# Two transformer blocks on one core: softmax totals from a column of ones, and outputs kept by tokens

## The chip, the core and the metric

The kernel runs on one core of one Trainium2 chip. The metric is the device time of one execution in microseconds (us). A core has five engines that this text speaks of: PE (TensorE, matmuls, with its weight loads shown apart as PEld), DVE (VectorE), ACT (ScalarE), POOL (GpSimd) and SP (SyncE, which issues most of the DMAs). PE writes its results to PSUM[...]; DVE and ACT read them there[...].

## The reference

The input `x` is 4 sequences (batch B = 4) of S = 1024 tokens with D = 128 features. Two blocks follow each other, each adding `s * g` to the residual stream `x`: `s` is an attention of 16 heads of 8 features, `g` is the silu of a feed-forward network, and both read the same layernorm of `x`. Cut to what matters:

```python
def block0_attention(x):             # causal window of 64 tokens
    k, q, v = split(x @ w_kqv)
    score = q @ k.T / sqrt(D) + alibi_bias        # -inf outside the window
    return softmax(score) @ v                     # by head

def block0_ffn(x):                   # an expert mixture per sequence
    g  = (relu(x @ gate_w1.T + gate_b1) @ gate_w2.T + gate_b2).mean(axis=1)
    W1 = W1 + sum_e g[e] * TW1[e];  b1 = b1 + g @ Tb1      # per sequence
    W2 = W2 + sum_e g[e] * TW2[e];  b2 = b2 + g @ Tb2
    return gelu(x @ W1.T + b1) @ W2.T + b2

def block1_attention(x):             # over the batch: 4 positions, 1024 columns
    q, k, v = x @ Wq.T + bq, x @ Wk.T + bk, x @ Wv.T + bv
    probs = softmax(q @ k.T + gate(q) * position_bias)
    return (probs @ v) @ Wo.T + bo

def block1_ffn(x):
    h = silu(x @ w1.T * w1_s) * (x @ w2.T * w2_s)
    h = gelu(h @ h1.T * h1_s)
    h = gelu(h @ h2.T * h2_s)
    return h @ w3.T * w3_s

xn = layernorm(x); x = x + block0_attention(xn) * silu(block0_ffn(xn))
xn = layernorm(x); x = x + block1_attention(xn) * silu(block1_ffn(xn))
```

All matmuls are in fp32.

## The kernel before

**Tiling.** The tokens are cut into eight units u of U = 512 tokens, two to a sequence. Activations lie by features: 128 features on the partitions, tokens along the free axis. Each unit goes through the first block (attention in four blocks t of 128 queries, and the feed-forward `hid0` and `out0`), then a residual step and a second layernorm, then the second feed-forward (`gated`, `hidden` twice, `out1`). The second attention mixes the four sequences, so it waits for the last of them and runs in eight slices of 128 columns (`attend`, steps with a star) beside unit 7.

**Order.** PE, ACT and DVE execute exactly the order of a long string, `ORDER`: each word is a step, a letter and its arguments, written out by hand. `q` projects queries, keys and values; `m` and `v` evacuate them; `s`, `b`, `x`, `o` are scores, bias, exponential, weighting of a block; `d` divides a pair of blocks by their totals; `A` to `E` are gates and the mixing of expert weights (`E` is one of 16 DVE steps for a sequence); `f`, `g` the first feed-forward; `r` the residual; `l` and `t` the statistics of first and second layernorm, `n` its scaling, `k` its way back to features; `w`, `h`, `i`, `j` the second feed-forward; `y` the last output. A step with several words per unit does a quarter of the work in each. POOL and SP are placed by the framework.

**Block-0 attention.** The scores of 16 heads stand in one PSUM tile of four banks, `ps_S` (L393). DVE adds bias and mask (L410), ACT takes the exponential without a maximum (L741; a second version of the program, with the maximum, exists behind a flag and isn't run here). `weighted` makes two sets of matmuls into `ps_O`: the value products (L438: 32 per block, each 64 queries, the 32-column stationary window of `vb` holding one head's 8 value columns per head group between zeros), and the softmax totals (L451: 16 or 32 per block, with a constant 0/1 matrix `totals` as stationary operand). Both come out by features: row = head and feature, column = query. `divided` takes the reciprocal of all 128x256 totals (L462) and multiplies (L463).

**Layernorm.** Its statistics need tokens on partitions. The first reads a second copy of the input that is loaded by tokens (`in_xt`, kept in `g1`), while `x` holds the copy by features. The second (`ln_mid`) turns `x` on PE by four transposes (L224, tile `ps_T`) first. `ln_back` (L231) turns the scaled tokens back to features for the matmuls.

**Outputs.** `out0` (L481), `out1` (L536; L531 in two halves for unit 7) and the second attention's `project_out` (L666) have the weights as stationary operand and 512 tokens moving past. Their results are by features, so biases and scales are per-partition operands of the ACT or DVE instruction that evacuates them.

**PSUM.** Besides `ps_S` there are three single-bank buffers `ps_M`, taken in turn by nearly all other matmuls, and one bank with the tag O for `ps_O`, `ps_T` and `ps_V`.

Of the kernel before, what the change touches and what calls it, by code (L numbers as in the profile page):

```python
# [29 lines left out]
C_ID, C_MP, C_SEL, C_EXP, C_TOT, C_TOF = np.cumsum([0, 128, 4, 64, 256, 128]).tolist()  # L30
C_N = C_TOF + 128
# [3 lines left out]
for _name, _n in (  # L35
    ("gb1", 1), ("gb2", 8), ("b1", 4), ("b2", 1), ("bq", 1), ("bk", 1), ("bv", 1), ("bo", 1),
    ("gW", 8), ("gb", 8), ("ga", 1), ("pb", 4), ("w1s", 4), ("w2s", 4), ("h1s", 4), ("h2s", 4), ("w3s", 1),
):
    VEC[_name] = (sum(n for _, n in VEC.values()), _n)
V_N = sum(n for _, n in VEC.values())  # L40


def constants():
# [13 lines left out]


    tot = np.tile((r[None, :] // 8 == g[:, None]).reshape(1, P), (P, 1))
    c[:, C_TOT:C_TOT + P] = tot  # L60
    c[:, C_TOF:C_TOF + P] = tot * (p[:, None] < W)
# [24 lines left out]

ORDER = """
    l1 n10
    q0 m03 m00 m01 z m02 s00 b00 k10 A00 A01 s01 B0 b01 v00 C0 D0 E0 v01 s02 v03 x01 E0 E0 v02 E0 E0 x00 b02
    o00 s03 E0 x02 E0 l3 E0 E0 b03 o01 E0 f0 d01 E0 f1 E0 x03 E0 f0 f0 E0 E0 f1 E0 l2 o02 o03 n30 f0 d03 n20  # L90
    g0 g0
    q1 v11 k20 k30 r0 t0 f1 m11 A10 n01 m12 g1 k01 v10 f1 v13 w0 m13 g1 m10 v12 w0 w0 s10 A11 b10 w0 s11 x10
    b11 x11 h0 h0 s12 o10 b12 o11 s13 b13 h0
    q2 d11 x12 h0 o12 B1 x13 C1 D1 E1 E1 E1 E1 i0 E1 o13 E1 d13 i0 E1 E1 i0 E1 E1 r1 i0 E1 E1 t1 E1 f2 E1 j0
    v20 v23 j0 f2 f2 E1 m21 m20 E1 n11 g2 v21 f2 k11 m22 g2 v22 w1 m23 w1 s20 w1 b20 w1 h1 l4 x20 h1 s21 n40
    o20 b21 x21 h1 o21 s22 d21 b22 h1 x22 l5 i1 i1 s23 b23 o22 x23 n50 i1 i1 o23 j1 j1 k50 f3 d23
    q3 r2 t2 m31 n21 f3 k40 f3 v31 f3 g3 m30 A20 k21 v32 v33 g3 w2 v30 w2 m32 m33 w2 A21 s30 b30 w2 x30 B2
    h2 s31 o30 b31 C2 x31 h2 s32 o31 D2 h2 E2 b32 h2 x32 E2 i2 d31 i2 E2 o32 E2 E2 E2 s33 E2 E2 b33 E2 x33
    E2 i2 E2 i2 E2 o33 E2 d33
    q4 f4 r3 E2 E2 m43 E2 f4 j2 v40 t3 n31 f4 m41 f4 j2 g4 k31 v42 m40 v43 g4 w3 w3 m42 l6 v41 w3 w3 s40 b40  # L100
    n60 h3 x40 h3 s41 b41 o40 k60 l7 n70 h3 x41 h3 k70 s42 o41 b42 i3 f5 i3 s43 b43 d41 x43 x42 i3 i3 o42
    o43 j3 d43 j3 r4
    q5 t4 f5 m53 f5 n41 A30 m51 m50 f5 v51 g5 k41 g5 v53 w4 m52 v52 v50 w4 w4 s50 b50 w4 x50 A31 h4 h4 B3
    o50 s51 b51 C3 x51 h4 D3 E3 E3 E3 s52 b52 E3 E3 E3 E3 o51 x52 h4 i4 d51 s53 b53 E3 E3 E3 E3 o52 x53 i4
    i4 E3 i4 o53 d53 E3 r5 j4 f6 E3 E3
    q6 f6 t5 m61 E3 f6 m63 f6 n51 v60 j4 v61 g6 k51 g6 v62 w5 m62 v63 w5 m60 w5 w5 s60 b60 h5 x60 h5 s61 o60
    b61 x61 h5 h5 o61 s62 i5 i5 b62 d61 x62 i5 s63 b63 x63 i5 o62 o63 d63 f7 r6 f7 j5 f7 t6 j5 n61 f7
    q7 k61 m71 m70 g7 v70 v73 v71 w6 m72 g7 m73 w6 v72 *A0 w6 s70 *B0 b70 *V0 w6 s71 b71 x70 h6 *A1 *b0 s72
    b72 x71 *C0 *E0 *B1 *N0 x72 o70 h6 *b1 *D0 o71 *A2 d71 *V1 *C1 *B2 o72 s73 *E1 *N1 h6 *G0 b73 *F0 *b2 h6
    *D1 x73 *C2 i6 *E2 o73 i6 *G1 d73 r7 *Y0 *A3 *N2 t7 *V2 *B3 *D2 *b3 n71 *V3 i6 i6 *C3 *E3 *F1 k71 j6 *N3  # L110
    *Y1 w7 *G2 *D3 j6 w7 w7 *A4 *F2 *G3 *F3 *Y2 *Y3 y60 *V5 *B4 *b4 *A5 *A6 w7 *V6 *V4 *C4 *B5 *E4 *b5 *V7
    h7 *B6 *A7 h7 *b6 *N4 *C5 *B7 *b7 *D4 h7 *C7 *E5 h7 *G4 *E7 *F4 *N5 *Y4 *D5 *G5 i7 *C6 *E6 *N6 i7 *F5
    *N7 *D6 *Y5 i7 *D7 *G6 i7 *F6 *G7 j7 *Y6 j7 *F7 y70 *Y7 y71
# [4 lines left out]
def block_kernel(ctx: ExitStack, tc: tile.TileContext, a: dict, out: bass.AP):  # L118
# [20 lines left out]

    x = main.tile([P, B, S], F32, tag="x", name="x")  # L140

    g1 = main.tile([P, B, S], F32, tag="g1", name="g1")
    xt = [g1[:, b, :].rearrange("p (i d) -> p i d", d=P) for b in range(B)]
# [7 lines left out]
    tb = const.tile([P, FC + 1, E], F32, tag="tb", name="tb")  # L151
# [6 lines left out]
    nc.scalar.dma_start(out=g1[:, 0, 0:U], in_=a["xt"][:, 0:U])  # L158
    nc.sync.dma_start(out=wqkv, in_=a["wqkv"])
    nc.sync.dma_start(out=cst, in_=a["const"])  # L160
    nc.scalar.dma_start(out=g1[:, 0, U:S], in_=a["xt"][:, U:S])
# [15 lines left out]
    totals = [cst[:, at:at + P].rearrange("p (g c) -> p g c", g=4) for at in (C_TOT, C_TOF)]  # L177
# [7 lines left out]
    DVE.memset(vb[:, 0:2328], 0.0)  # L185
    POOL.memset(vb[:, 2328:24 + 9 * 512], 0.0)
    slots = vb[:, 24:24 + 9 * 512].rearrange("p (m h q) -> p m h q", m=9, h=H)[:, :, :, 0:HD]

    def tokens(u):

        b, c = u // 2, (u % 2) * U
        return b, slice(c, c + U)

# [21 lines left out]
    def ln_in(u):  # L215

        return ln_stats(xt[u // 2][:, 4 * (u % 2):4 * (u % 2) + 4, :])

    def ln_mid(u):

        b, cx = tokens(u)
        turned = ps.tile([P, 4, P], F32, tag="O", name="ps_T")
        for i in range(4):
            PE.transpose(turned[:, i, :], x[:, b, cx.start + i * P:cx.start + (i + 1) * P], ident)  # L224
        return ln_stats(turned)
# [32 lines left out]

    one = const.tile([P, 1], F32, tag="one", name="one")
    POOL.memset(one, 1.0)  # L260
    in_order = {mybir.EngineType.PE, mybir.EngineType.Activation, mybir.EngineType.DVE}
    with tc.manual_schedule(engines=in_order | {mybir.EngineType.Pool}):
        steps = bound()

        for i in range(3):
            PE.matmul(bank(), lhsT=vb[:, 0:P], rhs=vb[:, 0:U], start=True, stop=True)
            if i == 1:
                next(steps)
        scale = ln_in(0)
        next(steps)  # L270
        fast = nc.values_load(flag[0:1, 0:1], min_val=0, max_val=1)
        ln_back(0, scale())

    def program(exact):
# [41 lines left out]
        def gates_c(b, gr):  # L316
            shares = small([P, FC + 1, E], "shares")
            DVE.tensor_tensor(shares, tb, gr.unsqueeze(1).to_broadcast([P, FC + 1, E]), ALU.mult)
            mb = at.tile([P, FC + 1], F32, tag="mb", name="mb", bufs=2)
            DVE.tensor_reduce(mb, shares, AX.X, ALU.add)  # L320
            DVE.tensor_tensor(mb, mb, v("b1", 0, FC + 1), ALU.add)
            own = [at.tile([P, F], F32, tag=f"mw{j}", name=f"mw{j}", bufs=2) for j in range(2)]
            mixed[b] = (own[0], own[1], mb)

# [27 lines left out]
        def qkv(u):  # L352
# [26 lines left out]
            def value(i):  # L379
                copy = DVE.tensor_copy if u else ACT.copy  # L380
                rows, first = ((slice(0, W), 0), (slice(0, W), 1), (slice(W, P), 1), (slice(W, P), 2))[i]
                copy(slots[rows, first:first + 7:2], src[rows])
# [45 lines left out]
        def weighted(u, t, pr):  # L428

            if t % 2 == 0:  # L430
                put(("op", u), ps.tile([P, 2, 2 * P], F32, tag="O", name="ps_O"))
            op = made["op", u][:, :, (t % 2) * P:(t % 2) * P + P]
            for i in range(2):
                qs = slice(W * i, W * i + W)
                at0 = 24 + 512 * (2 * t + i)
                for g in range(4):
                    for j in range(4):
                        PE.matmul(  # L438
                            op[32 * j:32 * j + 32, 0, qs],
                            lhsT=vb[:, at0 + 128 * j + 24 * g:at0 + 128 * j + 24 * g + 32],  # L440
                            rhs=pr[:, j, g, qs],
                            start=(g == 0),
                            stop=(g == 3),
                        )
            spans = ((slice(0, P), 0),)
            if u % 2 == 0 and t == 0:
                spans = ((slice(0, W), 1), (slice(W, P), 0))
            for qs, first in spans:
                for g in range(4):
                    for j in range(4):  # L450
                        PE.matmul(  # L451
                            op[32 * j:32 * j + 32, 1, qs],
                            lhsT=totals[first][:, g, :],
                            rhs=pr[:, j, g, qs],
                            start=(g == 0),
                            stop=(g == 3),
                        )

        def divided(t, op, s):

            inv = small([P, 2 * P], "inv")
            DVE.reciprocal(inv, op[:, 1, :])  # L462
            DVE.tensor_tensor(s[:, (t - 1) * P:(t + 1) * P], op[:, 0, :], inv, ALU.mult)  # L463
# [12 lines left out]
        def out0(u, hid):  # L476
            b, _ = tokens(u)
            _, m2, mb = mixed[b]
            op = bank()
            for c in range(FC):  # L480
                PE.matmul(op, lhsT=m2[:, c * P:(c + 1) * P], rhs=hid[:, c, :], start=(c == 0), stop=(c == FC - 1))  # L481
                if c == 1:
                    yield None
            g = tmp.tile([P, U], F32, tag="g", name="g", bufs=1)
            ACT.activation(g, op, AF.Silu, bias=mb[:, FC:FC + 1])  # L485
            yield g

        def residual(u, g, s):
            b, cx = tokens(u)
            POOL.tensor_tensor(g, g, s, ALU.mult)  # L490
            POOL.tensor_tensor(x[:, b, cx], x[:, b, cx], g, ALU.add)
# [32 lines left out]
        def out1(u, hid):  # L524

            b, cx = tokens(u)
            if u == 7:
                for r in (slice(0, U // 2), slice(U // 2, U)):
                    op = bank()
                    for i in range(FC):  # L530
# [344 lines left out]
```

## Time and profile before

| | |
|---|---|
| median of 3 runs (lowest to highest) | 586.19 us (586.15 to 586.88) |
| the profiled execution: its own time | 588.99 us |
| its span in the profile | 587.1 us |
| mean granted PE clock | 0.984 of full speed |
| instructions | 12660 |
| HBM read, written | 26.37 MB, 2.10 MB |
| DMA, slices 1 to 3 of 40 (the first 44 us) | 306 to 400 GB/s |
| PE busy, 0 to 45 us / 45 to 560 us / 560 to 588 us | 31.6 / 512.8 / 20.4 us |

The profile shows one execution. The busy time of an engine is the part of the span in which it worked. A group's line gives the source line, engine and operation, output and inputs with partitions by elements, the count, the busy time in us with the mean of one in ns, and then the engine's idle time just before that group with what ended it. The chain that ended last is followed back from the last instruction: at each step to what released it. Its pieces in order of time read: start in us, length in us, engine, tile, line, count. An fp32 matmul is two records in all these counts, a transpose one. Matmul ends are modelled, so a group's mean is longer than what one matmul adds when many follow each other.

### The profile page before, as it was taken

The page shows a single profiled execution, that of the slowest core. Times are in us where ns is not written, and L with a number is a line of the kernel's source. Part 1 is how long each engine was busy: PE and PEld are TensorE (multiplying, and loading weights), DVE is VectorE, ACT ScalarE, POOL GpSimd, SP SyncE. Part 2 cuts the span into 40 slices and gives each one's busy share as a digit, 9 for nine tenths or more (in the row PEclk, how much of TensorE's full clock was granted, in tenths as well). Part 3 has the DMA queues.
Part 4 walks back from the last instruction along what each step waited for, and adds up shares of the span by engine and source line. Part 5 has one row for each costly group of instructions (what it writes and reads, how often), then busy time and mean ns, then how long its engine had stood idle before and what let it go on. Part 6 is the DMA issues. An engine that isn't in the chain of part 4 may idle for free.

```text
span 587.1 us, 12660 instructions
## 1 busy us (share of the span) xinstructions
PE 564.8 (96%) x5608; PEld 287.5 (49%) x5608; DVE 333.9 (57%) x545; ACT 334.2 (57%) x380; POOL 110.6 (19%) x123
## 2 busy tenths in 40 slices
PE   6589999999999999999999999999999999999995
PEld 2356455535455454545554554445554555444443
DVE  5876535755333473663325384743146768878764
ACT  2546757286655736556566564664866747345441
POOL 3012000211002000211010000300021334557433
PEclk8869999999999999999999999999999999999999
DMA  8980000620000012400000032000000000001002
GB/s 306 400 343 2 2 2 3 213 74 2 1 2 0 1 52 95 145 2 1 1 2 1 1 109 73 0 1 2 2 2 1 2 2 11 5 27 33 1 15 64
DMA packets 10750, 29.35 MB, mean 50 GB/s; under 512 B 1216, under 2 KB 4800, under 8 KB 9664
## 3 DMA queue, kind: packets, MB, share of 16 engines
q1 hardware_dynamic: 10256, 26.90, 12.9%
q10 hardware_dynamic: 432, 1.57, 0.7%
q8 instruction: 46, 0.75, 0.5%
q14 instruction: 16, 0.13, 0.1%
HBM read 26.37 MB, written 2.10 MB: 48 GB/s over the span
## 4 chain that ended last, share of the span: by engine, by line
PE 93%; ACT 2%; DMA 1%; DVE 1%; issue 1%; POOL 0%; ACTq 0%; DVEq 0%
PE ps_M L520 38%; PE ps_O L438 6%; PE ps_S L393 6%; PE ps_O L451 5%; PE ps_M L481 5%; PE ps_M L508 4%; PE ps_M L472 4%; PE ps_M L509 4%; PE ps_M L536 4%; PE ps_M L569 4%; PE ps_S L648 1%; PE ps_M L617 1%; PE ps_M L231 1%; PE ps_S L364 1%; PE ps_S L361 1%
## 5 line engine op out<-in xcount | busy, mean ns | idle before, releaser
L520 PE MATMUL ps_M<-big,l1h 128*128 128x512 f32 x512 | 229.6, 598 | 0.0
L520 PEld LDWEIGHTS ps_M<-big,l1h 128*128 128x128 f32 x512 | 94.6, 190 | 115.1 <-issue 110.8
L410 DVE TENSOR_TENSOR big<-ps_S,bias 128x2048 f32<-128x2048 f32 x32 | 73.3, 2290 | 94.9 <-PE ps_S L393 78.0
L521 ACT ACTIVATE big<-ps_M,vec 128x512 f32<-128x512 f32 x64 | 43.9, 687 | 109.1 <-PE ps_M L520 108.7
L741 ACT ACTIVATE big<-big 128x2048 f32<-128x2048 f32 x32 | 61.0, 1910 | 15.4 <-DVE big L410 15.1
L462 DVE RECIPROCAL inv<-ps_O 128x256 f32<-128x256 f32 x16 | 28.1, 1754 | 37.0 <-PE ps_O L451 36.9
L521 ACT ACT_TABLE_LOAD x35 | 44.9, 1283 | 5.6 <-PE ps_M L520 5.0
L490 POOL TENSOR_TENSOR g<-g,s 128x512 f32<-128x512 f32 x8 | 10.8, 1353 | 184.1 <-DVE s L463 179.7
L512 DVE SCALAR_TENSOR_TENSOR big<-ps_M,vec,t2k 128x512 f32<-128x512 f32 x32 | 23.9, 748 | 32.6 <-PE ps_M L509 16.5
L438 PEld LDWEIGHTS ps_O<-big,vb 128*32 128x32 f32 x2048 | 32.3, 114 | 19.6 <-issue 15.0
L438 PE MATMUL ps_O<-big,vb 128*32 128x64 f32 x2048 | 37.5, 226 | 3.9 <-ACT big L741 3.4
L451 PE MATMUL ps_O<-big,cst 128*32 128x128 f32 (+1 forms) x1152 | 36.5, 269 | 3.2 <-issue 3.2
L393 PE MATMUL ps_S<-qm,k 32*64 32x256 f32 (+1 forms) x768 | 36.9, 472 | 2.5 <-DVE big L410 2.5
L330 DVE SCALAR_TENSOR_TENSOR mw<-tw,gr,mw 128x512 f32<-128x512 f32 x42 | 35.1, 836 | 1.2
L741 ACT ACT_TABLE_LOAD x26 | 33.4, 1283 | 3.3 <-DVE big L410 2.9
L508 PE MATMUL ps_M<-xn,l1w 128*128 128x512 f32 x64 | 33.4, 603 | 1.2 <-ACT g L485 1.2
L509 PE MATMUL ps_M<-xn,l1w 128*128 128x512 f32 x64 | 32.9, 595 | 0.0
L473 ACT ACTIVATE big<-ps_M,mb 128x512 f32<-128x512 f32 x32 | 21.7, 687 | 18.8 <-PE ps_M L472 18.5
L511 ACT ACTIVATE t2k<-ps_M,vec 128x512 f32<-128x512 f32 x32 | 22.0, 686 | 17.8 <-PE ps_M L508 17.3
L472 PE MATMUL ps_M<-xn,mw 128*128 128x512 f32 x64 | 31.2, 597 | 0.0
L451 PEld LDWEIGHTS ps_O<-big,cst 128*32 128x32 f32 x1152 | 29.3, 115 | 3.9 <-issue 3.8
L393 PEld LDWEIGHTS ps_S<-qm,k 32*64 32x64 f32 x768 | 18.9, 133 | 24.2 <-issue 11.0
(148 smaller groups left out, 687.0 us busy)
## 6 DMA issues: line engine op xcount, KB each, us to landing
tw<-in_tw SPq DMA_DIRECT2D x24, 512.0 KB, 4.1
big<-in_tw SPq DMA_DIRECT2D x4, 1024.0 KB, 8.2
l1h<-in_l1h SPq DMA_DIRECT2D x2, 1024.0 KB, 15.3
g<-in_xt SPq DMA_DIRECT2D x3, 512.0 KB, 12.1
x<-in_x SPq DMA_DIRECT2D x1, 1536.0 KB, 14.2
out<-t2k SPq DMA_DIRECT2D x8, 192.0 KB, 2.1
bias<-in_bias ACTq DMA_DIRECT2D x1, 1024.0 KB, 7.9
l1w<-in_l1w SPq DMA_DIRECT2D x3, 256.0 KB, 13.9
```

Source lines behind the costliest of these rows:

```text
L330: DVE.scalar_tensor_tensor(m, more[e // 2][:, e % 2, :], gr[:, e:e + 1], base if e == 0 else m, ALU.mult, ALU.add)
L393: PE.matmul(sp[rows, j, :, q0:q0 + n], lhsT=k[r, key:key + W], rhs=qm[r, :, t * P + q0:t * P + q0 + n], start=True, stop=True,)
L410: DVE.tensor_tensor(pr, sp, bias, ALU.add)
L438: PE.matmul(op[32 * j:32 * j + 32, 0, qs], lhsT=vb[:, at0 + 128 * j + 24 * g:at0 + 128 * j + 24 * g + 32], rhs=pr[:, j, g, qs], start=(g = ...
L451: PE.matmul(op[32 * j:32 * j + 32, 1, qs], lhsT=totals[first][:, g, :], rhs=pr[:, j, g, qs], start=(g == 0), stop=(g == 3),)
L472: PE.matmul(hp, lhsT=m1[:, c * P:(c + 1) * P], rhs=xn[:, b, cx], start=True, stop=True)
L481: PE.matmul(op, lhsT=m2[:, c * P:(c + 1) * P], rhs=hid[:, c, :], start=(c == 0), stop=(c == FC - 1))
L508: PE.matmul(p1, lhsT=wt["w1"][:, c * P:(c + 1) * P], rhs=xn[:, b, cx], start=True, stop=True)
L509: PE.matmul(p2, lhsT=wt["w2"][:, c * P:(c + 1) * P], rhs=xn[:, b, cx], start=True, stop=True)
L520: PE.matmul(hp, lhsT=wt[name][:, i, c * P:(c + 1) * P], rhs=hid[:, i, :], start=(i == 0), stop=(i == FC - 1))
L521: ACT.activation(new[:, c, :], hp, AF.Gelu, scale=v(name + "s", c))
L741: ACT.activation(pr, pr, AF.Exp)
```

## The change

- **Totals.** Each head's 8 value columns in `vb` get a ninth behind them that holds ones. The window of 32 columns then yields, for each query, a head's weighted values and its total in one matmul. Three of the four head groups use windows 27 columns wide in effect (three heads of 9); the fourth group of both blocks of a pair shares a third region of `ps_O`, which is now 3 x 128 columns. The matmuls of `totals` and the constants for them go.
- **By tokens.** After a pair of blocks ACT copies `ps_O` to SBUF (step `c`, `taken`), PE turns its three parts (step `p`, `turned`, into a `ps_M` bank), and `divided` works on tokens: reciprocals of 24 and 8 totals per token, two multiplications.
- `out0`, `out1` and `project_out` take slices of 128 tokens as stationary operand, and the weights move. Their results are by tokens; biases become rows: `row_weights` once, `row_bias` (step `H`) for each sequence, `bo` as a row added by DVE, and the scale of `w3` multiplied into the weights by POOL (step `Z`).
- The residual stream `x` and the gate `g1` are by tokens. `ln_mid` and its transposes go; both layernorms read `x`. The second copy of the input is no longer loaded. The output is written by tokens.
- `ORDER` is a new one throughout.

```diff
-    nc.scalar.dma_start(out=g1[:, 0, 0:U], in_=a["xt"][:, 0:U])
+    nc.scalar.dma_start(out=x[:, 0, 0:U], in_=a["x"][:, 0:U])
...
+    nc.sync.dma_start(out=sb, in_=a["sb"])
...
-    DVE.memset(vb[:, 0:2328], 0.0)
+    DVE.memset(vb[:, 0:U], 0.0)
+    DVE.memset(vb[:, U:2328], 0.0)
...
+    POOL.memset(slots[:, :, :, HD], 1.0)
+    def row_weights():
+        rp = bank((P, 4, P))
+        for i in range(2):
+            PE.matmul(rp[:, i, :], lhsT=sb[:, i * P:(i + 1) * P], rhs=sb[:, 2 * P:3 * P], start=True, stop=True)
+        DVE.tensor_scalar(wb[:, 0, :], rp[:, 0, :], 1.0 / S, None, ALU.mult)
+        DVE.tensor_copy(wb[:, 1, :], rp[:, 1, :])
...
+        def row_bias(hrep):
+            rp = bank()
+            PE.matmul(rp[:, 0:D], lhsT=hrep, rhs=wb[:, 0, :], start=True, stop=True)
+            row = at.tile([P, D], F32, tag="row", name="row")
+            DVE.tensor_tensor(row, rp[:, 0:D], wb[:, 1, :], ALU.add)
+            return row
...
             if t % 2 == 0:
-                put(("op", u), ps.tile([P, 2, 2 * P], F32, tag="O", name="ps_O"))
+                put(("op", u), ps.tile([P, 3, P], F32, tag="O", name="ps_O"))
...
                 for g in range(4):
+                    part, row = (odd, 9 * g) if g < 3 else (2, 9 * odd)
                     for j in range(4):
+                        col = at0 + 128 * j + 32 * g - row
                         PE.matmul(
-                            op[32 * j:32 * j + 32, 0, qs],
-                            lhsT=vb[:, at0 + 128 * j + 24 * g:at0 + 128 * j + 24 * g + 32],
+                            op[32 * j:32 * j + 32, part, qs],
+                            lhsT=vb[:, col:col + 32],
                             rhs=pr[:, j, g, qs],
...
-            for qs, first in spans:
-                for g in range(4):
-                    for j in range(4):
-                        PE.matmul(
-                            op[32 * j:32 * j + 32, 1, qs],
-                            lhsT=totals[first][:, g, :],
-                            rhs=pr[:, j, g, qs],
...
+        def taken(u, op):
+            ab = tmp.tile([P, 3, P], F32, tag="ab", name="ab", bufs=1)
+            ACT.copy(ab, op)
+            return ab
+
+        def turned(ab):
+            tp = bank((P, 4, P))
+            for i in range(3):
+                PE.transpose(tp[:, i, :], ab[:, i, :], ident)
+            return tp
...
-            DVE.reciprocal(inv, op[:, 1, :])
-            DVE.tensor_tensor(s[:, (t - 1) * P:(t + 1) * P], op[:, 0, :], inv, ALU.mult)
+            DVE.reciprocal(i3, most[:, :, :, HD])
+            DVE.reciprocal(i1, rest[:, :, :, HD])
...
-                PE.matmul(op, lhsT=m2[:, c * P:(c + 1) * P], rhs=hid[:, c, :], start=(c == 0), stop=(c == FC - 1))
+                for i in range(4):
+                    PE.matmul(op[:, i, :], lhsT=hid[:, c, i * P:(i + 1) * P], rhs=m2[:, c * D:(c + 1) * D], start=(c + i == 0), stop=(c + i == FC + 2))
...
-            ACT.activation(g, op, AF.Silu, bias=mb[:, FC:FC + 1])
+            DVE.tensor_tensor(g, op, made["row", b].unsqueeze(1).to_broadcast([P, 4, D]), ALU.add)
+            ACT.activation(g, g, AF.Silu)
...
-                PE.matmul(op, lhsT=wt["w3"][:, i, :], rhs=hid[:, i, :], start=(i == 0), stop=(i == FC - 1))
+                    for k in range(n):
+                        at0 = (r + k) * P
+                        PE.matmul(op[:, k, :], lhsT=hid[:, i, at0:at0 + P], rhs=wt["w3"][:, i, :], start=(i + k == 0), stop=(i + k == FC + n - 2))
...
-                PE.matmul(op, lhsT=wa[:, 3 * D:4 * D], rhs=xn[:, :, cx], start=True, stop=True)
+                for t in range(B):
+                    PE.matmul(op[:, t, :], lhsT=xn[:, t, cx], rhs=wa[:, 3 * D:4 * D], start=True, stop=True)
...
-                DVE.scalar_tensor_tensor(y, op[:, 0:n, :], v("bo"), g1[:, 0:n, cx], ALU.add, ALU.mult)
-                DVE.tensor_scalar(xn[:, n, cx], op[:, n, :], v("bo"), None, ALU.add)
+                DVE.tensor_tensor(xn[:, :, cx], op, v("bo", 0, D).unsqueeze(1).to_broadcast([P, B, D]), ALU.add)
+                DVE.tensor_tensor(y, xn[:, 0:n, cx], g1[:, 0:n, cx], ALU.mult)
```

The order, by the example of units 1 and 2 around the new steps:

```diff
-    b11 x11 h0 h0 s12 o10 b12 o11 s13 b13 h0
-    q2 d11 x12 h0 o12 B1 x13 C1 D1 E1 E1 E1 E1 i0 E1 o13 E1 d13 i0 E1 E1 i0 E1 E1 r1 i0 E1 E1 t1 E1 f2 E1 j0
+    b11 s12 x11 h0 o10 b12 o11 c11 s13 b13 h0 p11 d11
+    q2 x12 h0 B1 x13 o12 C1 D1 E1 i0 o13 E1 E1 c13 E1 E1 H1 m20 p13 d13 i0 E1 r1 E1 E1 m21 i0 i0 j0 t1 j0 E1
```

## The prediction

> **What bounds the kernel now.** I read the page first: its busy times, then its chain of waits, then its groups of instructions.
>
> ```profile
> PE 564.8 (96%) x5608; PEld 287.5 (49%) x5608; DVE 333.9 (57%) x545; ACT 334.2 (57%) x380; POOL 110.6 (19%) x123
> PE 93%; ACT 2%; DMA 1%; DVE 1%; issue 1%; POOL 0%; ACTq 0%; DVEq 0%
> L451 PE MATMUL ps_O<-big,cst 128*32 128x128 f32 (+1 forms) x1152 | 36.5, 269 | 3.2 <-issue 3.2
> L462 DVE RECIPROCAL inv<-ps_O 128x256 f32<-128x256 f32 x16 | 28.1, 1754 | 37.0 <-PE ps_O L451 36.9
> ```
>
> PE is busy 96% of the span and makes 93% of the chain that ended last; DVE and ACT have over 250 us free each. So work taken from PE shortens the kernel by what it occupies on the chain, and work given to DVE, ACT or POOL costs nothing where they keep up. The line to look at is L451, the totals; the reciprocal L462 is long (1754 ns), but off the chain.
>
> A mean of a group includes a matmul's pipelined end, so the prices come from the chain in order of time, where each piece is what it adds:
>
> ```profile
> 45.38 0.87 PE ps_O L451 x32
> 53.77 0.86 PE ps_S L362 x2
> 54.63 0.89 PE ps_S L364 x8
> 97.17 1.03 PE ps_O L438 x64
> 115.33 0.44 PE ps_T L224 x4
> 178.24 0.44 PE ps_M L231 x4
> ```
>
> One fp32 matmul is two records. Read: one pass of totals is 0.87 us; a 128x512 matmul 0.86; **the same work as four 128x128 matmuls, each with new weights, 0.89** (L364, the values); the value products of one 128-query block 1.03; a 128x128 transpose, one record, 0.11. L451's share of the chain is 5.2%, 30.5 us.
>
> Last the first 47 us, the one stretch where PE isn't full: the chain there, and how busy the engines are.
>
> ```profile
> 29.44 1.34 PE ps_O L451 x49
> 30.78 2.47 issue
> 33.24 0.65 PE ps_O L451 x15
> 16.96:46.74 29.78, 20.87 (x434) 13.64 (x436) 24.73 (x36) 16.77 (x18) 2.39 (x4) 0.77 0.84 334
> ```
>
> From the first bias addition to the last E0, DVE is busy 24.7 of 29.8 us (third busy column), with sixteen mixing steps at 0.75; DMA is 0.84 full.
>
> [...] L364's records follow at 0.89/8 = 0.111 us, although a load row reads 192 ns. [...]
>
> **The change part by part.**
>
> *Totals (L451) go.* The value products stay at 64 records of 64 columns for each block; only their window of `vb` moves. In units 1 to 7 28 passes of 0.87 to 0.89 go: 24.6 us. In unit 0 L451 holds 5.5 us of the chain, its pieces summed, under a slow clock. Not all of that comes back: the E0s must be through before out0, and DVE has 5.1 us idle in that stretch. I take 4.0. **-28.6.** The 2.47 us before L451's last records (released by nothing shown) I count at zero: under the same DMA load it may meet the next instruction instead.
>
> *Middle layernorm reads tokens.* Eight groups of four transposes L224 go: seven of 0.44 and one of 0.65. **-3.7.** Its statistics then read SBUF: L210 345 ns for 404, 1.9 us of DVE in all, hidden.
>
> *Copy, turn, divide.* 16 pairs of blocks get an ACT copy 128x384 (between 417 at 256 and 582 at 512: about 0.5, sum 8, hidden by ACT's free 250 us), three transposes, and four small DVE operations. PE: 48 x 0.11 = **+5.3.** DVE: reciprocals of 24 and 8 elements by the line through L637 (64: 553) and L462 (256: 1754) 0.30 and 0.20; [...] 1.08 for 2.18 before, -17.6. A new wait stands here: PE's transposes wait for ACT's copy, and all PE work is queued behind. The order puts PE work between "c" and "p" nearly everywhere: f1 (0.86), f0 g0 g0 k30, h0 (3.43), f4. The thinnest is the end of unit 2, with only H1 (0.3) against a 0.5 us copy. That is below 0.5 us of wait a time; I take 0, and 16 x 0.5 = 8 as upper end. None comes out below zero. Division done late holds a `ps_M` bank, one of three; the order has "d" next to "p", so 0.
>
> *Out0, out1 and the last projection by tokens.* 32 + 32 + 8 matmuls of 512 columns become four of 128 (unit 7's halves of out1 two each): 72 x (0.89 - 0.86) = **+2.2.** The lower end is 0; the upper is the first rival on the other side.
>
> *Biases.* Four `row_bias` matmuls at 0.32 (the like of L311 on the chain): **+1.3**. Two in `row_weights` at the start, under a slow clock, half in a 0.7 us gap that PE has there: **+0.5**. DVE gets 8 additions of 512 (0.69) before the silu, 5.5, and 8 x 0.3 in `gated_out`; beside the 17.6 and 1.9 saved DVE still ends lower, so hidden. Only the last `gated_out` lies in the tail: **+0.3**. out0's bank is now freed by DVE, not by a silu behind a 1283 ns table load, for which PE waited 1.2 us in all (L508 on L485): possible gain up to 1.2, counted as 0.
>
> *Loads.* The second copy of the input goes (2 MB, at 400 GB/s 5 us of DMA), and 128 KB of constants; SP gets one more small issue (0.4) behind the constants and two fewer later. Nothing on the chain after 5.4 us waits for a load, so 0; up to -2 if the 2.47 us was DMA's doing. POOL: one 128x512 product for w3 (1.3 us), a ones fill; POOL is 19% busy and the product is needed two units later: 0. The split memset lets warm-up matmuls begin earlier; the first real PE work waits for the layernorm: 0. The new order otherwise costs 0 as long as no engine waits longer: PE idles 22 us now, nearly all in the first 47 us and the tail, so little is to be had.
>
> Sum: -28.6 - 3.7 + 5.3 + 2.2 + 1.3 + 0.5 + 0.3 = **-22.7**. The profiled execution took 588.99 (span 587.1, 1.9 around it), 2.8 above the median shown, 586.19; a difference carries over: 586.2 - 22.7 = **563.5**.
>
> **Rivals.**
>
> *More comes back at the start (557.5).* If the 2.47 us vanishes, unit 0's totals return whole (1.5) and the bank waits go (1.2), it is 5 to 6 more. For it: the input's second copy no longer competes. Against: DVE's 24.7 us of work there.
>
> *The hand-off stalls PE (571.5).* [...] a copy behind an exponential (1.9) or a table load (1.28) comes late, and PE stands. At 0.5 for each of 16 pairs it is +8. For it: until now no PE instruction waited for anything that came out of `ps_O`. Against: PE work lies between in nearly all places.
>
> *Slower: weight loads become the bound.* out0, out1 and the projection make (128+128+32) x 2 = 576 records with a load each. If loads don't hide and each record costs its load row, 0.190 instead of 0.111, that is +45: 609. It decides from 22.7/576 = 39 ns extra, 0.150 a record. The place is out0 and out1; against it stands L364, the same shape, at 0.111.
>
> *It doesn't do what it says:* if the new order gave PE as much waiting as L451 gave it work, 586. Nothing in the profile points to it.
>
> **Numbers.** Forecast 0.69, more at the start 0.12, hand-off 0.14, weight loads 0.03, no change 0.01, an unforeseen slowdown 0.01. 0.2% (1.2 us) is about what a measurement can tell from no change. Faster 0.95, same 0.01, slower 0.04. The range takes the start's gain and most of the hand-off: 556 to 573.
>
> **What would show it.** L451 and `ps_T` gone; PE busy about 540; a group of 48 transposes at 0.33 a triple on the chain; out0 and out1 pieces of 8 records at 0.89; DVE busy lower by some 10 us. It is wrong if PE idles more than now after 50 us, above all ahead of the new transposes or of the out0 matmuls, or if 8 records of out1 take over 1.2 us.

## The result, and the profile after

The changed kernel takes **564.62 us** (median of 4 runs, 563.96 to 566.32) against 586.27 before: ratio 0.9633, 95% interval 0.9611 to 0.9655, some 21.6 us less. Run again beside the experiments it took 564.87 (ratio 0.9623, 0.9601 to 0.9644). The forecast was 563.5. The profiled execution took 564.78, with a span of 563.0. The profiled execution of before lay 2.7 us over its median, so the two profiles, 24.1 us apart in span, overstate the gain by about that much; sums over runs below go by medians.

From the page of the changed kernel: busy times, shares of the chain, and the groups of the division's reciprocal, the value products and the two feed-forward outputs (out-in, count, then busy us and mean ns, then idle before and its releaser):

```profile
PE 541.0 (96%) x4908; PEld 299.0 (53%) x4908; DVE 324.0 (58%) x592; ACT 332.5 (59%) x391; POOL 113.6 (20%) x125
...
PE 86%; DVE 8%; ACT 2%; POOL 1%; issue 1%; DVEq 0%; ACTq 0%; POOLq 0%
...
L480 DVE RECIPROCAL inv<-ps_M 128x24 f32<-128x24 f32 x16 | 4.9, 306 | 63.2 <-PE ps_M L470 63.2
...
L453 PE MATMUL ps_O<-big,vb 128*32 128x64 f32 x2048 | 35.9, 226 | 2.7 <-ACT big L760 2.7
...
L560 PE MATMUL ps_M<-l1w,big 128*128 128x128 f32 x256 | 31.2, 276 | 0.0
L507 PE MATMUL ps_M<-mw,big 128*128 128x128 f32 x256 | 30.9, 275 | 0.0
```

The group of totals and the tile `ps_T` are gone. PE is as full as before, 96%, with 23.8 us less work; its idle time is 22.0 us, as it was (22.3). PE's share of the chain fell from 93% to 86% and DVE's rose from 1% to 8%: between 15 and 47 us the chain now runs in large part through DVE's mixing steps and bias additions (L342 and L422, 37% of it there). DVE's busy time fell by 9.9, about the 10 that the prediction gave. The reciprocal of 24 takes 306 ns where 0.30 us was worked out, that of 8 takes 145 ns where 0.20 was. The products of 192 and 64 take 357 and 213 ns; the line through two products of the kernel before (L463, 424 ns at 256; L662, 684 at 512) gives 359 and 229 as an estimate. All four make 1.02 us; the 1.08 of the prediction holds the author's own estimate for the two products.

The chain in order of time (start, length, tile, line, count), one pair of blocks and one unit's outputs:

```profile
76.23 1.93 PE ps_O L453 x128
...
82.84 0.33 PE ps_M L470 x3
...
84.88 0.89 PE ps_S L376 x8
...
106.63 3.59 PE ps_M L560 x32
...
114.59 1.78 PE ps_M L507 x16
...
118.10 1.78 PE ps_M L507 x16
```

Two blocks of value products now follow each other with nothing between, and with the ones column in them they cost no more than before (1.93 for both, where one took 1.03); three transposes cost 0.33. A unit's out1 is 3.59 for 32 records, 0.112 each; out0 two halves of 1.78. The price taken from the values (0.111 a record; 0.89 for eight) was right.

### The profile page after: what moved, and what is told of

The parts are those of the page before. It is cut to its first block, busy times and chain, and to the rows that moved or that the text cites. A ratio compares the mean times of both kernels' runs of the same rounds, so it can differ in the third digit from the quotient of the medians.

```text
span 563.0 us, 11321 instructions
## 1 busy us (share of the span) xinstructions
PE 541.0 (96%) x4908; PEld 299.0 (53%) x4908; DVE 324.0 (58%) x592; ACT 332.5 (59%) x391; POOL 113.6 (20%) x125
## 4 chain that ended last, share of the span: by engine, by line
PE 86%; DVE 8%; ACT 2%; POOL 1%; issue 1%; DVEq 0%; ACTq 0%; POOLq 0%
PE ps_M L547 38%; PE ps_S L405 6%; PE ps_O L453 5%; PE ps_M L535 5%; PE ps_M L536 5%; PE ps_M L507 5%; PE ps_M L496 4%; PE ps_M L560 4%; PE ps_M L593 3%; PE ps_S L672 1%; PE ps_M L226 1%; DVE mw L342 1%; PE ps_M L641 1%; PE ps_M L470 1%; PE ps_S L376 1%
## 5 line engine op out<-in xcount | busy, mean ns | idle before, releaser
L422 DVE TENSOR_TENSOR big<-ps_S,bias 128x2048 f32<-128x2048 f32 x32 | 73.3, 2290 | 71.8 <-PE ps_S L405 58.7
L480 DVE RECIPROCAL inv<-ps_M 128x24 f32<-128x24 f32 x16 | 4.9, 306 | 63.2 <-PE ps_M L470 63.2
L453 PE MATMUL ps_O<-big,vb 128*32 128x64 f32 x2048 | 35.9, 226 | 2.7 <-ACT big L760 2.7
L342 DVE SCALAR_TENSOR_TENSOR mw<-tw,gr,mw 128x512 f32<-128x512 f32 x42 | 34.6, 825 | 1.2 <-DMA tw<-in_tw 0.2
L496 PE MATMUL ps_M<-xn,mw 128*128 128x512 f32 x64 | 32.0, 607 | 1.7 <-DVE s L487 0.9
L560 PEld LDWEIGHTS ps_M<-l1w,big 128*128 128x128 f32 x256 | 30.5, 192 | 4.7 <-issue 3.9
L507 PEld LDWEIGHTS ps_M<-mw,big 128*128 128x128 f32 x256 | 30.3, 192 | 4.4 <-issue 3.0
L560 PE MATMUL ps_M<-l1w,big 128*128 128x128 f32 x256 | 31.2, 276 | 0.0
L507 PE MATMUL ps_M<-mw,big 128*128 128x128 f32 x256 | 30.9, 275 | 0.0
## 6 DMA issues: line engine op xcount, KB each, us to landing
x<-in_x SPq DMA_DIRECT2D x1, 1024.0 KB, 14.5
```

The source lines that it names most:

```text
L342: DVE.scalar_tensor_tensor(m, more[e // 2][:, e % 2, :], gr[:, e:e + 1], base if e == 0 else m, ALU.mult, ALU.add)
L422: DVE.tensor_tensor(pr, sp, bias, ALU.add)
L453: PE.matmul(op[32 * j:32 * j + 32, part, qs], lhsT=vb[:, col:col + 32], rhs=pr[:, j, g, qs], start=(odd + i + g == 0), stop=(odd + i + g = ...
L496: PE.matmul(hp, lhsT=m1[:, c * P:(c + 1) * P], rhs=xn[:, b, cx], start=True, stop=True)
L507: PE.matmul(op[:, i, :], lhsT=hid[:, c, i * P:(i + 1) * P], rhs=m2[:, c * D:(c + 1) * D], start=(c + i == 0), stop=(c + i == FC + 2))
L560: PE.matmul(op[:, k, :], lhsT=hid[:, i, at0:at0 + P], rhs=wt["w3"][:, i, :], start=(i + k == 0), stop=(i + k == FC + n - 2))
```

## The experiments

All are edits of the changed kernel except the last. Differences are medians against its 564.87 us. The half-width of each ratio is about 0.002, 1.2 us, so a difference of two runs is good to about 1.7 us. "Before", run beside each group of them, took 586.5 to 586.7.

| run | us | ratio to before (95%) | against the changed kernel |
|---|---|---|---|
| totals put back | 595.38 | 1.0144 (1.0124 to 1.0165) | +30.5 |
| transposes of the middle layernorm back | 567.21 | 0.967 (0.9652 to 0.9687) | +2.3 |
| outputs 512 wide | 562.83 | 0.959 (0.9572 to 0.9607) | -2.0 |
| no turn | 560.05 | 0.9542 (0.9524 to 0.9559) | -4.8 |
| old order, hand-off tight | 593.82 | 1.012 (1.0097 to 1.0142) | +29.0 |
| second input load back | 564.67 | 0.962 (0.9599 to 0.9641) | -0.2 |
| ones written later | 564.26 | 0.9613 (0.9592 to 0.9634) | -0.6 |
| no bias row | 564.62 | 0.9625 (0.9604 to 0.9647) | -0.3 |
| new order, p right behind c | 585.34 | 0.9965 (0.9948 to 0.9982) | +20.5 |
| old order, hand-off spaced | 579.34 | 0.9871 (0.9849 to 0.9892) | +14.5 |
| kernel before without totals | 558.72 | 0.9514 (0.9492 to 0.9535) | 27.8 below before by medians, 28.5 by the ratio |

### The terms of the sum, one at a time

**The totals, put back.**

```diff
+            spans = (slice(0, P),)
...
+            for qs in spans:
+                for g in range(4):
+                    for j in range(4):
+                        PE.matmul(op[32 * j:32 * j + 32, 3, qs], lhsT=cst[:, 32 * g:32 * g + 32],
+                                  rhs=pr[:, j, g, qs], start=False, stop=(odd == 1 and g == 3))
```

(Where the kernel before had two spans, in an even unit's first block, this run has two as well; `ps_O` gets a fourth part for the sums.)

> The changed kernel with the 16 or 32 totals matmuls of each block put back, into a free quarter of ps_O that nobody reads; no other edit. Sum-of-PE theory: every pass is paid on PE's chain: 28 x 0.88 = 24.6 us after unit 0 and 4.0 to 5.5 in unit 0, so 593 to 595 us (28.6 to 30 over the changed kernel). Waiting theory (the new order left PE waits that the old totals used to fill): part of them hides, 585 or less. If the start of the kernel is set by DVE, unit 1 begins less than 5.5 us later than in the changed kernel (47.1).

It took 30.5 us more: nothing of a pass is hidden, and the waiting theory falls. The chain of this run also shows a stretch that I had put down to chance:

```profile
32.26 0.64 PE ps_O L466 x19
32.90 3.10 issue
36.00 0.66 PE ps_O L466 x13
```

In the middle of a block's totals PE again stands for 3.1 us, and nothing shown releases it. The kernel before has this (2.47), this run has it, and the other twelve traces, all of kernels without totals, have no such wait before a matmul; the one with the second input load put back has none either. So it goes with the totals at the start, and not with that load; what it is, the traces don't say. Unit 1's first projection begins at 52.0 here and at 47.1 in the changed kernel: 4.9 of the 30.5 lie in unit 0.

**The totals, taken out of the kernel before**, with nothing else changed.

```diff
-            for qs, first in spans:
...
-            DVE.reciprocal(inv, op[:, 1, :])
+            DVE.reciprocal(inv, op[:, 0, :])
```

> The kernel before without the totals matmuls, nothing else changed but that the reciprocal is taken of the value sums instead, so the softmax is left undivided in effect. My sum: 24.6 after unit 0 plus 4.0 in it, 28.6 less: 558. If putting them back in the changed kernel (30.3 more) is the right size: 556. If the order of before then waits elsewhere: 560 or more.

28.5 us less by the ratio (27.3 to 29.8), 27.8 by medians: the predicted 28.6 within the error. In the two traces, 29.8 us apart in span, unit 1 begins at 46.5 for 52.8: 6.3 at the start and 23.5 in the rest, where 4.0 and 24.6 were predicted. But PE's granted clock differs there. From 30 to 47 us (window, its length, busy us with counts of PE, PEld, DVE, ACT and POOL, granted clock, DMA share, GB/s), first before, then without totals:

```profile
30.00:47.00 17.00, 13.98 (x310) 9.28 (x305) 13.25 (x24) 8.65 (x7) 1.95 (x2) 0.74 0.70 281
30.00:47.00 17.00, 14.34 (x238) 7.41 (x223) 16.72 (x37) 12.66 (x13) 3.22 (x4) 0.95 0.68 275
```

The profiled execution of before lay 2.7 us over its median, so a part of the 6.3 may belong to that one execution. In the other pair, totals put back against the changed kernel, the clock was 0.90 and 0.91, so the 4.9 found there is the cleaner figure, although that profile too lay 2.4 us over its median. In the prediction's window (16.96 to 46.74 us) DVE has become the full engine:

```profile
16.96:46.74 29.78, 21.02 (x357) 11.43 (x356) 28.20 (x49) 20.94 (x24) 3.51 (x5) 0.89 0.83 337
```

**The transposes of the middle layernorm.**

```diff
         def stats(u, i):
+            if i == 1:
+                turned_x = ps.tile([P, 4, P], F32, tag="O", name="ps_T")
+                for k in range(4):
+                    PE.transpose(turned_x[:, k, :], cst[:, 0:P], ident)
```

> The changed kernel with four transposes put back ahead of each middle layernorm, of a constant and into the bank of ps_O, read by nobody, so that they wait for no residual. Sum-of-PE theory: 8 x 0.44 = 3.5 us, so 568.1. Waiting theory: hidden, 564.6. A mechanism beyond the matmuls (ps_O's single bank taken at a bad moment): over 570.

2.3 us more: within the error of about 1.7 it agrees with 3.5, and it is clear of 0 and of 5.

**Wide outputs.**

```diff
-                    PE.matmul(op[:, i, :], lhsT=hid[:, c, i * P:(i + 1) * P], rhs=m2[:, c * D:(c + 1) * D], ...)
+                PE.matmul(op.rearrange("p i d -> p (i d)"), lhsT=m2[:, c * D:(c + 1) * D], rhs=hid[:, c, :], ...)
```

(out1 and `project_out` alike.)

> The changed kernel with out0, out1 and project_out issued as before: weights stationary, 512 tokens moving (256 in unit 7's out1), into the same banks; their results come out by features, so the output's values are not the reference's. Sum-of-PE theory: 72 x 0.03 = 2.2 us less, 562.4. Weight-load theory (a 128-column record costs 0.15 or more): 22 us less or beyond, 542. No cost at all: 564.6.

2.0 us less, where 2.2 was worked out; PE's busy time is 2.4 less (537.1 for 539.5 in the rerun). The weight loads of 576 narrow records are hidden (records follow at 0.112 in the changed kernel, where a load row of L560 or L507 reads 192 ns): the forecast's rival on the slower side is refuted, since it needed 22.

**No turn.**

```diff
-            ACT.copy(ab, op)
+            ACT.activation(ab, op, AF.Copy, bias=1.0)
...
-            put(("tp", u, t), turned(made["ab", u, t]))
+            put(("tp", u, t), made["ab", u, t])
```

> The changed kernel without the three transposes of each pair of blocks: ACT's copy stays (with 1 added, so that no reciprocal of zero arises), and DVE divides the copy as it stands, by features, so the output's values are not the reference's. Sum-of-PE theory: 48 x 0.11 = 5.3 us less, 559.3. Hand-off theory (PE waits for the copy): 5.3 plus up to 8 less, 551. The trace of the changed kernel shows 0.2 us of such waits, so I expect 559.

4.8 less: the transposes' own 5.3 within the error, and no hidden wait beside them.

**Edits counted at nothing.** The second input load is two DMAs into `g1`; without the row, the silu reads `op`:

```diff
+        nc.sync.dma_start(out=g1[:, 0, :], in_=a["x"][:, 0:S])
...
+        nc.sync.dma_start(out=g1[:, 1:B, :].rearrange("p b s -> p (b s)"), in_=a["x"][:, S:B * S])
```

```diff
-            DVE.tensor_tensor(g, op, made["row", b].unsqueeze(1).to_broadcast([P, 4, D]), ALU.add)
-            ACT.activation(g, g, AF.Silu)
+            ACT.activation(g, op, AF.Silu)
```

> The changed kernel with a second copy of the input loaded into g1 in the first 44 us, 2 MB more on SP's queue, at the places where the kernel before had such loads; g1 is overwritten later. Theory that loads are off the chain: 564.6 to 565. Theory that DMA traffic held the engines up at the start (the 2.47 us before the last totals of block 1): 1 to 3 us slower.

> The changed kernel without the addition of the bias row after out0: the silu reads PSUM directly, so the bias b2 of the first feed-forward is left out. DVE loses 8 x 0.69 us, and out0's bank is freed by ACT, behind a table load, as before. Theory that this DVE work is hidden: 564.9, as the changed kernel. Theory that freeing the bank by DVE is a gain: up to 1.2 us slower, 566. Theory that the row's addition lies on the chain somewhere: up to 2 us faster.

-0.2 and -0.3 us, no difference. The 2 MB that are no longer loaded are worth nothing that could be measured, although the DMA share in the changed kernel's trace is 1.01 from 15 to 30 us, at 418 GB/s; and neither the 5.5 us of additions on DVE nor the earlier freeing of out0's bank can be seen. PE's waits for that bank (L508 on L485, 1.2 us before) are gone from both lists, with the addition and without it, so it isn't the addition that removed them.

**Ones written later.** A term that the prediction missed. It said that the split memset lets the warm-up matmuls begin earlier, and cost that at 0. In the changed kernel's list of PE's waits (waiter, releaser, total us, times, longest):

```profile
PE ps_M L270 <- POOL vb L254: 3.8, 1, 3.8
...
PE ps_M L593 <- DVE s L487: 1.0, 1, 1.0
PE ps_M L496 <- DVE s L487: 0.9, 1, 0.9
...
PE ps_M L470 <- ACT ab L464: 0.2, 1, 0.2
```

The warm-up (L270) waits for POOL's fill of ones, which comes after both memsets, and starts at 3.80 for 3.33 before; the bound's matmul, the flag and the first scaling queue behind it (9.22 for 8.86).

```diff
-    POOL.memset(slots[:, :, :, HD], 1.0)
...
         fast = nc.values_load(flag[0:1, 0:1], min_val=0, max_val=1)
+        POOL.memset(slots[:, :, :, HD], 1.0)
         ln_back(0, scale())
```

> The changed kernel with the fill of ones in vb moved behind the warm-up matmuls on POOL. In the trace of the changed kernel the warm-up waits 3.8 us for that fill, L243 for the warm-up, DVE's flag for L243, and the first scaling of the layernorm for the flag (9.22 us), while its rstd is ready at 8.13. Start-chain theory: 1.0 us less. If DVE's mixing steps set the end of the start, 0.

The first scaling then starts at 7.48, not 9.22. In this trace the 1.7 us are kept: unit 1 begins at 45.4 for 47.1, unit 7 at 406.7 for 408.4, and the span is 561.5 for 563.0; DVE's mixing steps come earlier by as much, so they took nothing of it back. But the profiled execution was the fastest of five (563.28). The median is only 0.6 us lower, with intervals that overlap. How much of the 1.7 other executions keep, and why, is open; this version is not shown to beat the change.

### The hand-off and the order

**p right behind c**, in the new order, nothing else moved (`... o01 b03 c01 p01 E0 f1 d01 ...`).

```diff
-    E0 v02 l3 E0 x00 E0 o00 x02 E0 E0 s03 o01 b03 c01 E0 f1 p01 d01
+    E0 v02 l3 E0 x00 E0 o00 x02 E0 E0 s03 o01 b03 c01 p01 E0 f1 d01
```

> The changed kernel with one edit to its order: each p stands right behind its c, so that PE comes to the transposes with nothing between them and the last value product. In the old order with the hand-off put in tightly PE waited 16.3 us for the copy, 13 times, 1.25 each. Hand-off theory: 16 x 1.0 to 1.25 = 16 to 20 us slower, 581 to 585. If that order was slow for other reasons and a copy costs only its 0.5 us: 8 us, 573.

20.5 us slower: nearly the whole gain is gone by moving 16 words. One line of its waits of PE, then a stretch of its chain:

```profile
PE ps_M L443 <- ACT ab L437: 15.2, 14, 2.5
```

```profile
77.70 2.00 PE ps_O L426 x128
79.70 0.02 issue
79.72 0.49 ACT ab L437
80.21 0.04 issue
80.25 0.55 PE ps_M L443 x3
80.80 1.05 PE ps_S L378 x16
```

Fourteen times PE waits for ACT's copy, 1.1 us each: the copy itself (0.49), and what ACT has in hand. Before the longest wait (2.48) the timeline has a table load and an activation ahead of the copy:

```profile
294.18 1.28 ACT L470 ACT_TABLE_LOAD   x1 [0.55 <-PE ps_M L469]
295.48 0.69 ACT L470 ACTIVATE big<-ps_M,mb 128x512 f32<-128x512 f32 x1
296.06 0.47 ACT L437 COPY ab<-ps_O 128x384 f32<-128x384 f32 x1
296.59 0.90 PE L443 MATMUL ps_M<-cst,ab 128*128 128x128 f32 x3 [2.48 <-ACT ab L437]
```

After a wait the transposes also take longer, 0.55 instead of 0.33, whether scores or a full-width matmul follow; in the changed kernel the one such wait (0.2, in the list above) stands between two full-width matmuls, and the same 0.55 follows it:

```profile
95.78 0.55 PE ps_M L470 x3
96.33 0.86 PE ps_M L547 x2
```

After the two longest waits (1.89 and 2.48) they take 0.82 and 0.90, and the granted clock is 0.66 and 0.70 in the 5 us after, for 1.00 and 0.97 in the 5 us before. So 15.2 of waiting and 3.7 of longer transposes make 18.9 of the 20.5.

**The old order**, first with c and p straight ahead of each d (tight, the lines with a minus), then with c behind the second value product and p and d at least one PE step later (spaced, the lines with a plus). Two places of many:

```diff
-    o13 E1 c13 p13 d13 i0 E1 E1 i0
+    o13 c13 E1 i0 E1 E1 i0 p13 d13
...
-    o23 j1 j1 k50 f3 c23 p23 d23
+    o23 c23 j1 j1 k50 f3 p23 d23
```

> The changed kernel with the order string of the kernel before; only the steps that did not exist are put in (c and p straight ahead of each d, H ahead of each D, Z ahead of the first w0). I counted the new order as worth 0. If that holds, apart from the 16 hand-offs, where PE now stands behind ACT's copy for about 0.5 to 0.8 us each since nothing lies between o, c and p, it is 8 to 13 us slower than the changed kernel: 573 to 578. If the order itself carries a good part of the gain (E0 against b02 at the start, divisions against bias additions), over 580. If the hand-offs cost nothing, 565.

> The changed kernel with the order of the kernel before, but with c behind the second value product of a pair and p and d one or more PE steps later (in three units the residual step moves behind d). Hand-off theory of the 29 us that the tight version cost: most of it goes; PE waits for the copy fall from 16.3 to under 3, 565 to 575. If the new order brings a gain of its own elsewhere: 580 or more.

The tight version lands in its second range (over 580), the spaced one between its two ranges. The tight version lost 29.0, of which PE's wait for the copy is 16.3:

```profile
PE ps_M L443 <- ACT ab L437: 16.3, 13, 2.9
```

Spaced, that wait is gone from its list, and 14.5 us remain. Its trace doesn't put them in one place: PE idles 33.1 us for 24.0 in the rerun of the changed kernel and is busy 5.0 us longer; the units' first projections fall behind step by step (49.1 for 47.1 in unit 1, 294.3 for 287.4 in unit 5, 419.2 for 408.4 in unit 7). So a changed kernel in the old order, as I adapted it, is still only 7.2 us better than before. With this layout, then, the order decides over much of the gain. Whether a better adaptation of the old order would keep it is open, and so is what a new order alone would bring the kernel before: no run tried either.

## Why the prediction was right

- **The sum.** Four large terms were measured alone: totals -27.8 by medians out of the kernel before (predicted -28.6), middle transposes -2.3 (-3.7), turn +4.8 (+5.3), narrow outputs +2.0 (+2.2). They make -23.3; the result, -21.6, leaves 1.7, where the prediction had 2.1 for row biases, row weights and tail, which were not measured one by one. With the totals as they cost in the changed kernel, 30.5, it leaves 4.4. Each term carries an error of over 1 us, so the sum closes to within a few us and not to tenths. PE's chain was the right account, and the pieces of the chain, not the groups' means, the right prices: 36.5 us busy for the totals, at a mean of 269 ns a record where a pass of 32 adds 0.87 us to the chain, would have overrated them. PE idles 2.6 us between 45 and 545 us, and idled 2.2 between 45 and 560 before, so the work taken from it came off the span.
- **Unit 0.** The step "I take 4.0" was probably too small: 4.9 came back in the changed kernel, and 6.3 in the kernel before, where the clock differed. The cap, DVE's 5.1 us of idle time, holds only up to the last E0 (46.74), while one pass of totals (47.55) lies wholly behind it. The later units' 24.6 was about right: 23.5 in the traces of the kernel before, and in the changed kernel 25.6 if 4.9 is taken from the 30.5 of the medians.
- **The 2.47 us without a releaser.** Counted at zero, "it may meet the next instruction instead". It met none: it vanished from the changed kernel and came back with the totals, as 3.1. Its share of the gain can't be told from the rest of unit 0. So parts of the rival "more comes back at the start" did come, and yet the time stayed at the forecast; what took them back isn't measured one by one.
- **The hand-off.** The forecast cost it at 0 because PE work lies between c and p; 0.2 us of waits show that to be right, and they stand where only H1 lies between, the place that it named the thinnest (it is the second pair of unit 1, not of unit 2). But the bound was wrong in size: "16 x 0.5 = 8 as upper end" took the copy's own length, and uncovered it is 20.5, since a copy also waits for what ACT is doing (1.28 and 0.69 us of it ahead of the copy at the longest wait), and the transposes are longer after a wait (0.55 for 0.33). The rival at 571.5 should have stood at 585, the edge of no gain at all.
- **The new order at 0.** As a cost it fits, since the sum closes without it; as an explanation it was too small. The order isn't a by-product: the same matmuls in the old order took 579 or 594 us.
- **Banks.** That a division gives its bank back in time ("so 0") failed in two places: PE waits 1.0 (L593) and 0.9 (L496) for a division to give back its `ps_M` bank, two lines of the list above.
- **The rest** held as far as it was tested: loads and bias row are hidden. The ones fill cost at most about 0.6 by medians, not told from nothing. Its wait (L270 on POOL's L254, 3.8 us) is for a fill of `vb`, which the diff shows.

In the tail `gated_out` grew by more than the 0.3 a slice that was taken. Its parts L696 and L698 are 684 and 954 ns on average, where the kernel before had L672 and L673 at 614 and 342: 0.68 more a slice. With L698 at its shortest, 0.56, it would be 0.29. That is off the chain in most slices; the addition at the very end (L713) isn't, and it took 1.10 us for 0.42 before, as the last section shows.

## What to carry to other kernels

On an engine that fills the chain, price an edit by the pieces of the chain in order of time. Work that rides in columns already paid for (a ones column in a padded window) was free here, 1.93 us for two blocks of value products where one took 1.03 before, while the passes it replaced had been paid in full (27.8 us out of the kernel before, 30.5 put back). A step that sends PE's result through another engine and back cost next to nothing here while other PE work stood between (0.2 us of waits), and 20.5 us without it: cost its uncovered size by what the other engine has in hand (1.1 us a wait), not by the copy's length (0.49). Judge a new layout together with an order made for it; in the two old ones tried here two thirds of the gain, or all of it, was gone.

## What the runs showed of the hardware

Three of DVE's lines in the traces of the two kernels, additions and products of two SBUF tiles, ran longer where a POOL operation on two tiles worked at the same time: L713 1.10 us for 0.43, L698 0.77 to 2.29 for 0.56, and L687 of the kernel before 1.02 for 0.43. In the changed kernel L713, an addition of 128x256, takes 0.43 us once and 1.10 the other time, at the very end; the rows of that timeline (start, length, engine) show POOL's addition L699 beside it:

```profile
552.38 0.43 DVE L713 TENSOR_TENSOR t2k<-t2k,x 128x256 f32<-128x256 f32 x1
...
556.67 1.05 POOL L699 TENSOR_TENSOR t2k<-t2k,x 128x384 f32<-128x384 f32 x1 [0.95 <-POOL t2k L699]
556.91 1.10 DVE L713 TENSOR_TENSOR t2k<-t2k,x 128x256 f32<-128x256 f32 x1
```

L698 takes between 0.56 and 2.29 us for one shape; 1.87 us of the longest lie beside POOL's L681:

```profile
543.86 2.36 POOL L681 TENSOR_TENSOR big<-big 128x1024 f32<-128x1024 f32 x1 [8.30 <-DVE big L680]
544.35 2.29 DVE L698 TENSOR_TENSOR t2k<-xn,g 128x384 f32<-128x384 f32 x1
```

All ten cases of these two lines in this trace fall alike. Four L698 and one L713 met no POOL operation and took 0.56 and 0.43; five met one and took 0.77 to 2.29. L712, a product of 128x256, overlapped the last L699 by 0.21 us only and took 0.42, as at 551.92 with no POOL operation beside it. The kernel before has it too, in its product L687, 1.02 us beside POOL's L674 and 0.43 alone:

```profile
578.25 1.00 POOL L674 TENSOR_TENSOR t2k<-t2k,x 128x384 f32<-128x384 f32 x1 [1.33 <-DVE t2k L672]
578.51 1.02 DVE L687 TENSOR_TENSOR t2k<-xn,g 128x256 f32<-128x256 f32 x1
...
582.54 0.43 DVE L687 TENSOR_TENSOR t2k<-xn,g 128x256 f32<-128x256 f32 x1 [1.07 <-DMA out<-t2k]
```

Before, the step that L696 and L698 do now read PSUM (L672) and took 608 to 618 ns, 0.62 beside POOL's L597 (at 522.60) and 0.61 with POOL idle (at 577.56). No experiment took POOL's work away to test this; it rests on the coincidence in these cases.
